# Null key's tables after the first entry's queries, in a decoder's cross-attention on one core

## The chip, the cores and the metric

The kernel runs on one core of a Trainium2 chip. The metric is device microseconds (us) of one launch on that core; lower is better. The engines are named as the profile names them: PE (TensorE, matrix products; PEld is its weight load), DVE (VectorE), ACT (ScalarE), POOL (GpSimd) and SP (SyncE, which here only issues DMAs). Each engine works through its own queue in order and waits at semaphores for the others.

## The reference, cut to what matters

Two decoder layers over 8 entries of 256 tokens with 256 features, float32. The change concerns the cross-attention of layer 1, with 16 heads of 64 and one learned "null" key and value that all heads share:

```python
q = split_heads(layernorm(x) @ Wq)                    # (8, 16, 256, 64)
k, v = split(ctx_2048 @ Wkv)                          # 256 context rows of 512
k = concat(null_kv[0], k); v = concat(null_kv[1], v)  # 257 keys
attn = softmax(q * 64**-0.5 @ k.T)
out = (attn @ v) @ Wout                               # 1024 -> 256
x = x + layernorm(out) * ln_scale + ln_bias
```

Before it stand layer 0 (self-attention with 16 heads of 16, a cross-attention, experts that choose their tokens) and layer 1's causal self-attention; behind it a feed-forward layer with one expert per token and a shared expert.

## The kernel before, in words

Everything is one program on one core. The tokens stay on the chip as `x`, 16 tiles of 128 tokens. A first stage works through 24 attention units (layer 0's self- and cross-attentions, layer 1's self-attentions) in an order written out by hand for all five engines (`order_of_jobs`, opened with `manual_schedule(engines=PINNED)`). Its last lines also make the first entry's keys and values for the heads of 64 (`keys_x`, `vals_x`; tiles kTx and vx), because these need only the context. The stage takes its on-chip memory from two pools (`pads`, `work` there called "aw") and its PSUM banks from three ("amm", "asc", "ao").

Then `order.close()` ends the hand-made order. Where no order is pinned, the framework's scheduler places each instruction on its engine's queue by program order and by when its inputs and its memory are free.

`tables_x` (called at L1085) makes three tables that all entries use, in tiles of a pool that lives to the end:

- `wn`: the query weights times the null key, summed over each head's 64 (DVE: two products `byk`, L829, four reductions, L836), so that the null key's scores are one product with the normalised tokens;
- `nvw`: the null value times the output weights, a row for each head. `nvs` holds for each pair of heads c (8 of them) a 128 x 128 block that is zero but for two columns; 8 products of 128 x 128 by 256 add up in one bank (L854), and DVE copies it out (L855);
- `hot8`: a table of ones for the sums of the weights.

`byk` and `nvs` are scratch tiles, in the slots of the tag "pT" of the pool that `work` names at that point.

After that the first stage's pools are closed (`first.close()`, `banks.close()`), and new ones are opened where those lay: "d2" for the work tiles, "wsum" for sums of weights, and the PSUM pools "xmm" (3 banks), "xsc", "xo".

`null_cross_attention` then makes entry 0's queries and runs over the 8 entries. For entry 0: `layernorm_T` (statistics, the norm `xn` on DVE, four PE transposes into PSUM, ACT's copy to `xnT`), `sums_of_weights` (DVE, L1406, tiles tw and twq: sums of blocks of the key, value and query weights, from which later entries' seven-product scheme takes its operands), `null_key` (two products with `wn`, then the exponential `en` on ACT), and `features` (the queries `qTx`: 16 products of 128 x 128 by 256, each in two halves of 64 columns by `product`, L272, four banks named fm, each copied out by the `copy` that is handed in). Then, for each entry, `weighted` computes scores (`stx`, L1513), exponentials (`pTx`, L1517), sums of weights (`den`, L1528) and weighted values (`ox`, L1553), while the next entry's keys, values and queries are made by `seven` (k7, v7, q7), and `outward` applies `wout_x` and adds `en` times `nvw`. From the second half of entry 0 on PE's order is again pinned.

A float32 product shows as two PE instructions in the trace. In a row such as "128*64 128x256" the first pair is contraction by weight columns, the second the moving operand. `product4` (L278) splits a product into four groups of 32 columns.

Of the kernel before, what the change touches and what calls it, by code (L numbers as in the profile page):

```python
# [43 lines left out]
HP = 32  # L44
CTX = 512
XH, XD = 16, 64
# [111 lines left out]
def plain(  # L158
# [4 lines left out]
    nc = tc.nc  # L163
# [79 lines left out]
    def norm_stats(views, eps, pool, tag):  # L243

        n = len(views)
        st = pool.tile([P, 2, 6], F32, tag=f"{tag}st", name=f"{tag}st")
        mv = pool.tile([P, 2, 2], F32, tag=f"{tag}mv", name=f"{tag}mv")
        for i, v in enumerate(views):
            nc.vector.bn_stats(st[:, i, :], v)
            nc.vector.bn_aggr(mv[:, i, :], st[:, i, :])  # L250
        ve = pool.tile([P, 2], F32, tag=f"{tag}ve", name=f"{tag}ve")
        nc.vector.tensor_scalar(ve[:, :n], mv[:, :n, 1], eps, None, ALU.add)  # L252
        rs = pool.tile([P, 2], F32, tag=f"{tag}rs", name=f"{tag}rs")
        nc.gpsimd.tensor_tensor(rs[:, :n], ve[:, :n], mhalf[:, :n], ALU.pow)  # L254
        return mv, rs

    def normed(dst, src, mv, rs, i, engine=nc.vector):
        return engine.tensor_scalar(dst, src, mv[:, i, 0:1], rs[:, i : i + 1], ALU.subtract, ALU.mult)

    def layernorm_T(b, work, mm, bufs=2):  # L260

        xn = work.tile([P, 2, D], F32, tag="xn", name="xn", bufs=bufs)
        mv, rs = norm_stats([x[:, 2 * b + t, :] for t in range(2)], 1e-5, small, "ln")
        for t in range(2):
            last = normed(xn[:, t, :], x[:, 2 * b + t, :], mv, rs, t)
        return last, transposed(xn, work, mm, "xnT", bufs=bufs)
# [3 lines left out]
    def product(out, lhsT, rhs, start, stop):  # L270
        return [
            nc.tensor.matmul(out[h], lhsT[:, h], rhs, start=start, stop=stop, skip_group_check=True)  # L272
            for h in (slice(0, 64), slice(64, P))
        ]
# [7 lines left out]
    def transposed(rows, work, mm, tag, dst=None, bufs=2):  # L282

        ps = mm.tile([P, 2, 2 * P], F32, tag="mm", name="tr")
        for t in range(2):
            for c in range(2):
                nc.tensor.transpose(ps[:, c, t * P : (t + 1) * P], rows[:, t, c * P : (c + 1) * P], ident)
        if dst is None:
            dst = work.tile([P, 2, 2 * P], F32, tag=tag, name=tag, bufs=bufs)
        nc.scalar.copy(dst, ps)  # L290
        return dst
# [285 lines left out]
    work = first.enter_context(tc.tile_pool(name="aw", bufs=2))  # L577
    banks = ExitStack()
    mm = banks.enter_context(tc.tile_pool(name="amm", bufs=3, space=PSUM))
# [214 lines left out]
    nc8 = XH // 2  # L794
# [24 lines left out]
        nc.sync.dma_start(lnb, a["L1_xattn_ln_bias"].rearrange("(o d) -> o d", o=1).to_broadcast([P, D]))  # L819
        return wd, ctxs, kvs, wproj, wkv_x, wq_x, wout_x, nkrow, nvcol, lns, lnb  # L820

    def tables_x(wd, wq_x, wout_x, nkrow, nvcol):


        wn = wd.tile([P, 2, 2, XD], F32, name="wn")
        nc.gpsimd.memset(wn, 0.0)
        for k in range(2):
            byk = work.tile([P, XH, XD], F32, tag="pT", name="byk", bufs=4)
            nc.vector.tensor_tensor(  # L829
                byk,  # L830
                wq_x[:, k, :].rearrange("p (h d) -> p h d", d=XD),
                nkrow.unsqueeze(1).to_broadcast([P, XH, XD]),
                ALU.mult,
            )
            for i in range(2):
                nc.vector.tensor_reduce(  # L836
                    wn[:, k, :, HP * i : HP * i + nc8 // 2],
                    byk.rearrange("p (c i g) d -> p i g c d", i=2, g=2)[:, i],
                    AX.X,
                    ALU.add,  # L840
                )

        own = wd.tile([P, 2], F32, name="own")
        nc.vector.tensor_reduce(own, ident.rearrange("p (g w) -> p g w", g=2), AX.X, ALU.add)
        nc.vector.tensor_tensor(own, own, nvcol.to_broadcast([P, 2]), ALU.mult)
        nvs = work.tile([P, nc8, P], F32, tag="pT", name="nvs", bufs=4)
        nc.gpsimd.memset(nvs, 0.0)
        for c in range(nc8):
            at = HP * (c % 2) + c // 2
            nc.vector.tensor_copy(nvs[:, c, at : at + XD + 1 : XD], own)  # L850
        nvw = wd.tile([P, D], F32, name="nvw")
        ps = mm.tile([P, 2, S], F32, tag="mm", name="nvw")
        for c in range(nc8):
            nc.tensor.matmul(ps[:, 0, :], nvs[:, c, :], wout_x[:, c, :], start=c == 0, stop=c == nc8 - 1)  # L854
        nc.vector.tensor_copy(nvw, ps[:, 0, :])  # L855

        hot = wd.tile([P, nc8, HP], F32, name="hot8")
        nc.gpsimd.memset(hot, 0.0)
        for i in range(2):
            nc.gpsimd.memset(hot.rearrange("p c w -> p (c w)")[:, HP * i : nc8 * HP : 2 * HP + 1], 1.0)  # L860
        return wn, nvw, hot
# [6 lines left out]
    def key_room():  # L868
        return kvs.tile([P, nc8, S], F32, tag="kT", name="kTx")

    def value_room():
        return kvs.tile([P, 2, XH, XD], F32, tag="vx", name="vx")
# [157 lines left out]
    order = ExitStack()  # L1030
# [19 lines left out]
    for n, u in enumerate(units):  # L1050
# [14 lines left out]
        for k in range(4):  # L1065
# [7 lines left out]
            if (n, k) == (20, 1):  # L1073
                for left in ex:
                    assert next(left, None) is None
                wd, ctxs, kvs, wproj, wkv_x, wq_x, wout_x, nkrow, nvcol, lns, lnb = weights_x()
# [5 lines left out]
    for i in (2, 3):  # L1082
        vals_x(kv0[1], ctxT0, i)
    order.close()
    wn, nvw, hot8 = tables_x(wd, wq_x, wout_x, nkrow, nvcol)  # L1085
    first.close()
    banks.close()
    banks = ExitStack()
    mm = banks.enter_context(tc.tile_pool(name="xmm", bufs=3, space=PSUM))
# [280 lines left out]
    def null_cross_attention(phase):  # L1370
        work = phase.enter_context(tc.tile_pool(name="d2", bufs=2))
# [3 lines left out]
        def features(dst, w, rows, copy):  # L1375
            n = w.shape[1]
            for c2 in range(0, nc8, 2):
                ps = mm.tile([P, 2, S], F32, tag="mm", name="fm")
                for i in range(2):
                    for cc in range(n):  # L1380
                        product(
                            ps[:, i, :], w[:, cc, (c2 + i) * P : (c2 + i + 1) * P], rows[:, cc, :], cc == 0, cc == n - 1
                        )
                copy(dst[:, c2 : c2 + 2, :], ps)

        def query_room():
            return work.tile([P, nc8, S], F32, tag="qT", name="qTx", bufs=1)
# [13 lines left out]
        def sums_of_weights(blocks, which):  # L1401
            ((b11, b12), (b21, b22)), (t1, t2, t3, t4) = blocks
            for dst, p, q in ((t1, b12, b11), (t2, b22, t1), (t4, b21, t2), (t3, b22, b12))[which]:
                for c in range(dst.shape[1]):
                    for m in range(dst.shape[2]):
                        nc.vector.tensor_tensor(dst[:, c, m], p[:, c, m], q[:, c, m], ALU.subtract)  # L1406
# [90 lines left out]
        def null_key(xnT):  # L1497
            nps = mm.tile([P, 2, S], F32, tag="mm", name="nps")
            for k in range(2):
                product(nps[:, 0, :], wn[:, k].rearrange("p g w -> p (g w)"), xnT[:, k, :], k == 0, k == 1)  # L1500
            en = work.tile([P, S], F32, tag="en", name="en")
            nc.scalar.activation(en, nps[:, 0, :], AF.Exp, scale=scale)
            return en
# [134 lines left out]
            return hidden_seven(q, shared["of_w"], sx, mm, pair, spare)  # L1638


        _, xnT = layernorm_T(0, work, mm, 1)
        (kT, v), qT = kv0, query_room()
        sums_of_weights(kv_blocks, slice(0, 3))
        sums_of_weights(q_blocks, slice(0, 3))
        en = null_key(xnT)
        features(qT, wq_x, xnT, nc.vector.tensor_copy)
        for blocks in (kv_blocks, q_blocks):
            sums_of_weights(blocks, slice(3, 4))
        load_router()
        order = ExitStack()  # L1650
        for b in range(B):
# [4 lines left out]
            if more:  # L1656
                _, xnT = layernorm_T(b + 1, work, mm, 1)
# [17 lines left out]
            if more:  # L1675
                of_x = sums_of_rows(xnT, 1, "swq", True)
                kT, v, qT = key_room(), value_room(), query_room()
# [24 lines left out]
            if more:  # L1702
# [4 lines left out]
                en = null_key(xnT)  # L1707
# [15 lines left out]
    with ExitStack() as phase:  # L1723
        null_cross_attention(phase)
# [1217 lines left out]
```

## Time and profile before

| | us |
|---|---|
| median of 3 runs | 1150.59 |
| lowest, highest | 1148.03, 1150.82 |
| the profiled execution | 1146.4 |
| its span, first to last instruction | 1144.7 |
| mean granted PE clock | 0.993 |

| engine | busy us in the span | share |
|---|---|---|
| PE | 1106.4 | 97% |
| DVE | 581.4 | 51% |
| ACT | 444.9 | 39% |
| POOL | 418.8 | 37% |

Times in rows are us from the span's start. A row of a timeline gives start, duration, engine, line, operation, what is written from what is read, shapes and count; in brackets stands the idle time of the engine before it, and what ended that. The chain of waits is the work that ended last, followed back from the last instruction; its rows give start, duration and what. Rows of stretches give for each stretch its length, then busy time (and instructions) of PE, PEld, DVE, ACT and POOL, then the granted PE clock, the DMA engines' busy share and GB/s. The edited part lies between 420 and 450 us.

### The profile page before, as it was taken

The page shows a single profiled execution, that of the slowest core. Times are in us where ns is not written, and L with a number is a line of the kernel's source. Part 1 is how long each engine was busy: PE and PEld are TensorE (multiplying, and loading weights), DVE is VectorE, ACT ScalarE, POOL GpSimd, SP SyncE. Part 2 cuts the span into 40 slices and gives each one's busy share as a digit, 9 for nine tenths or more (in the row PEclk, how much of TensorE's full clock was granted, in tenths as well). Part 3 has the DMA queues.
Part 4 walks back from the last instruction along what each step waited for, and adds up shares of the span by engine and source line. Part 5 has one row for each costly group of instructions (what it writes and reads, how often), then busy time and mean ns, then how long its engine had stood idle before and what let it go on. Part 6 is the DMA issues. An engine that isn't in the chain of part 4 may idle for free.

```text
span 1144.7 us, 33720 instructions
## 1 busy us (share of the span) xinstructions
PE 1106.4 (97%) x14690; PEld 704.9 (62%) x14690; DVE 581.4 (51%) x1577; ACT 444.9 (39%) x699; POOL 418.8 (37%) x480
## 2 busy tenths in 40 slices
PE   6979999999999999999999999999999999999997
PEld 3434455555555445767676767676765667888874
DVE  5557889899878447343433333332324573222213
ACT  4757776656444432232323323232414220222320
POOL 2427366446677422324141414142425223000014
PEclk9989999999999999999999999999999999999999
DMA  8073333231103200101010101010103026799934
GB/s 246 2 240 121 105 107 96 71 112 54 37 11 143 109 3 19 40 19 39 20 40 19 39 20 40 19 39 19 40 20 95 1 94 262 312 415 386 390 107 141
DMA packets 52253, 117.15 MB, mean 102 GB/s; under 512 B 8816, under 2 KB 37216, under 8 KB 47744
## 3 DMA queue, kind: packets, MB, share of 16 engines
q1 hardware_dynamic: 45920, 99.17, 25.4%
q0 software_dynamic: 3456, 12.73, 3.1%
q10 hardware_dynamic: 2720, 3.02, 0.7%
q8 instruction: 117, 1.92, 0.7%
q14 instruction: 40, 0.33, 0.1%
HBM read 104.26 MB, written 27.93 MB: 115 GB/s over the span
## 4 chain that ended last, share of the span: by engine, by line
PE 86%; DVE 6%; ACT 3%; issue 1%; SPq 1%; DMA 1%; POOL 1%; ACTq 0%; DVEq 0%; POOLq 0%
PE h L272 7%; PE st L330 7%; PE k L272 7%; PE v L272 6%; PE wo L272 5%; PE o L367 5%; PE ox L1553 5%; PE stx L1513 5%; PE out L1930 4%; PE out L1747 4%; PE qk L278 3%; PE h L1161 3%; PE q L272 3%; ACT pT L341 2%; PE ao L278 2%; PE v L278 2%
## 5 line engine op out<-in xcount | busy, mean ns | idle before, releaser
L341 ACT ACTIVATE pT<-st 128x1024 f32<-128x1024 f32 (+1 forms) x128 | 110.5, 915 | 74.2 <-PE st L330 70.3
L367 PE MATMUL o<-pT,padv 128*32 128x256 f32 (+1 forms) x1536 | 96.4, 367 | 7.0 <-DVE by_q L383 5.5
L1519 POOL TENSOR_TENSOR both<-pTx 128x512 f32<-128x512 f32 x64 | 81.5, 1298 | 27.1 <-issue 23.8
L272 PE MATMUL h<-xrT,w 128*64 128x128 f32 (+1 forms) x1936 | 87.1, 250 | 0.5 <-issue 0.5
L272 PEld LDWEIGHTS h<-xrT,w 128*64 128x64 f32 x1936 | 84.6, 137 | 3.4 <-issue 1.1
L341 ACT ACTIVATE pT<-st,kbias 128x1024 f32<-128x1024 f32 x64 | 67.9, 1112 | 36.0 <-PE st L330 36.0
L1154 DVE TENSOR_TENSOR midr<-sl,h 128x128 f32<-128x128 f32 x102 | 29.4, 288 | 100.7 <-PE h L272 67.5
L367 PEld LDWEIGHTS o<-pT,padv 128*32 128x32 f32 x1536 | 44.6, 110 | 54.4 <-issue 18.9
L1517 ACT ACTIVATE pTx<-stx 128x1024 f32<-128x1024 f32 x64 | 62.1, 1022 | 40.7 <-PE stx L1513 35.7
L1153 ACT ACTIVATE sl<-h 128x128 f32<-128x128 f32 (+1 forms) x114 | 35.4, 311 | 94.8 <-PE h L272 55.8
L330 PE MATMUL st<-qm,kT 32*128 32x512 f32 (+1 forms) x512 | 67.3, 594 | 3.7 <-DVE seq L513 2.2
L254 POOL TENSOR_TENSOR lnrs<-lnve,mhalf 128x2 f32<-128x2 f32 x48 | 35.8, 749 | 91.8 <-DVE lnve L252 84.9
L278 PE MATMUL qk<-xnT,l_wqkv 128*32 128x256 f32 x1024 | 68.5, 391 | 0.0
L1513 PE MATMUL stx<-qTx,kTx 64*128 64x256 f32 x512 | 64.3, 391 | 2.5 <-ACT pTx L1517 2.5
L1553 PE MATMUL ox<-pTx,vx 128*32 128x256 f32 x1024 | 62.3, 380 | 0.0
L1608 POOL TENSOR_TENSOR oT<-oT,rs 128x512 f32<-128x512 f32 x30 | 37.7, 1287 | 65.7 <-DMA rs<-rd 65.7
L1513 PEld LDWEIGHTS stx<-qTx,kTx 64*128 64x128 f32 x512 | 46.1, 186 | 20.7 <-ACT pTx L1517 7.2
L272 PE MATMUL wo<-wout_x,oT 128*64 128x256 f32 x512 | 58.0, 379 | 0.0
L346 POOL TENSOR_SCALAR_AFFINE_SELECT pT<-pT 128x512 f32<-128x512 f32 x64 | 42.1, 672 | 41.4 <-ACT pT L341 41.1
L254 POOL TENSOR_TENSOR lxrs<-lxve,mhalf 128x2 f32<-128x2 f32 x8 | 5.6, 704 | 133.5 <-DVE sc L1292 103.3
L278 PEld LDWEIGHTS qk<-xnT,l_wqkv 128*32 128x32 f32 x1024 | 32.9, 113 | 26.9 <-issue 8.7
L1930 PE MATMUL out<-w,midr 128*64 128x256 f32 x408 | 47.5, 379 | 0.7 <-issue 0.7
(365 smaller groups left out, 2154.8 us busy)
## 6 DMA issues: line engine op xcount, KB each, us to landing
w<-packs SPq DMA_DIRECT2D x22, 1408.0 KB
w<-packs SPq DMA_DIRECT2D x22, 768.0 KB
rs<-rd SPq DMA_DIRECT2D x16, 512.0 KB
packs<-L_ffn_w_eDF SPq DMA_DIRECT2D x8, 704.0 KB
packs<-L_ffn_w_eDF SPq DMA_DIRECT2D x8, 640.0 KB
packs<-L_ffn_w_eFD SPq DMA_DIRECT2D x8, 640.0 KB
wkv_x<-L_xattn_Wkv POOLq DMA_DIRECT2D x1, 4096.0 KB, 16.9
ctxT<-ctx_T SPq DMA_DIRECT2D x8, 512.0 KB
```

The lines of the kernel that those rows point to most:

```text
L272: nc.tensor.matmul(out[h], lhsT[:, h], rhs, start=start, stop=stop, skip_group_check=True)
L278: nc.tensor.matmul(out[h : h + HP], lhsT[:, h : h + HP], rhs, start=start, stop=stop, skip_group_check=True)
L330: nc.tensor.matmul(st[:, r, :, :n], self.kT[rows, c, bass.ts(kt, P)], self.qm[rows, :, c, q0:], start=True, stop=True,)
L341: nc.scalar.activation(pT[:, :, :, :n], st[:, 2 * k : 2 * k + 2, :, :n], AF.Exp, scale=self.scale, **kb)
L346: nc.gpsimd.affine_select(out=pT[:, :, :, :P], in_=pT[:, :, :, :P], compare_op=ALU.is_ge, fill=0.0, base=0, pattern=[[0, 2], [0, 2], [1, P ...
L367: nc.tensor.matmul(o[HP * j : HP * j + HP, m, q0:], self.v_pad[:, kt, 8 * c + 2 * j + m, :], pTs[j // 2][:, j % 2, m, : S - q0], start=kt ...
L1513: nc.tensor.matmul(st[:, g, kt, :], kT[rows, c, bass.ts(kt, P)], qT[rows, c, :], start=True, stop=True)
L1517: nc.scalar.activation(pT, st, AF.Exp, scale=scale)
L1519: nc.gpsimd.tensor_tensor(both, pT[:, :, 0, :], pT[:, :, 1, :], ALU.add)
L1553: nc.tensor.matmul(o[at : at + HP, i, :], v[:, kt, 2 * (c2 + i) + g, lo : lo + HP], pT[:, g, kt, :], start=kt == 0, stop=kt == 1, skip_gro ...
L1747: nc.tensor.matmul(ps, mid[:, i, lo : lo + P], w2[:, i, :], start=i == 0, stop=i == NFC - 1)
L1930: nc.tensor.matmul(ps[h], mid[:, i, h], sets[k % len(sets)][1][:, i, :], start=i == 0, stop=i == NFC - 1, skip_group_check=True,)
```

## The change

- `tables_x` is called inside `null_cross_attention`, after entry 0's norm and queries, and takes that stage's `work` and `mm`; so `byk` and `nvs` are tiles of "d2" and nvw's bank is one of "xmm".
- The products for `nvw` write only the 32 rows in which a pair's block is not zero: for each c two products of 128 x 32 by 256, for g = 0 and 1, at rows 64 g + 32 (c mod 2). Sixteen products of 32 columns take the place of eight of 128.
- Entry 0's queries are copied out of PSUM by ACT, not by DVE.
- In program order it is now: norm, queries, tables, null key, and then the sums of weights, which stood ahead of the null key and the queries. PE's order is pinned over norm, queries, tables and null key.

```diff
-    def tables_x(wd, wq_x, wout_x, nkrow, nvcol):
+    def tables_x(wd, wq_x, wout_x, nkrow, nvcol, work, mm):
...
         ps = mm.tile([P, 2, S], F32, tag="mm", name="nvw")
         for c in range(nc8):
-            nc.tensor.matmul(ps[:, 0, :], nvs[:, c, :], wout_x[:, c, :], start=c == 0, stop=c == nc8 - 1)
+            for g in range(2):
+                at = XD * g + HP * (c % 2)
+                nc.tensor.matmul(
+                    ps[at : at + HP, 0, :],
+                    nvs[:, c, at : at + HP],
+                    wout_x[:, c, :],
+                    start=c < 2,
+                    stop=c >= nc8 - 2,
+                    skip_group_check=True,
+                )
         nc.vector.tensor_copy(nvw, ps[:, 0, :])
...
     order.close()
-    wn, nvw, hot8 = tables_x(wd, wq_x, wout_x, nkrow, nvcol)
     first.close()
...
+        order = ExitStack()
+        order.enter_context(tc.manual_schedule(engines={mybir.EngineType.PE}))
         _, xnT = layernorm_T(0, work, mm, 1)
         (kT, v), qT = kv0, query_room()
+        features(qT, wq_x, xnT, nc.scalar.copy)
+        wn, nvw, hot8 = tables_x(wd, wq_x, wout_x, nkrow, nvcol, work, mm)
+        en = null_key(xnT)
+        order.close()
         sums_of_weights(kv_blocks, slice(0, 3))
         sums_of_weights(q_blocks, slice(0, 3))
-        en = null_key(xnT)
-        features(qT, wq_x, xnT, nc.vector.tensor_copy)
         for blocks in (kv_blocks, q_blocks):
             sums_of_weights(blocks, slice(3, 4))
```

## The prediction

> **What bounds the kernel now.** I read the page first: TensorE (PE) is busy 97% of the span, and the chain that ended last is 86% PE.
>
> ```profile
> PE 1106.4 (97%) x14690; PEld 704.9 (62%) x14690; DVE 581.4 (51%) x1577; ACT 444.9 (39%) x699; POOL 418.8 (37%) x480
> ```
>
> So an edit is worth what it takes off PE's row of work or out of a gap in it, and I looked for the place in the chain in order of time. The edited stretch runs from the last product of the first stage's values (vps, end 432.95) to the first score (stx):
>
> ```profile
> 425.01 1.07 PE ao L278 x16
> 426.09 6.87 PE vps L278 x64
> 432.95 3.67 PE nvw L854 x16
> ...
> 437.64 0.64 PE tr L287 x4
> ...
> 438.43 0.59 ACT xnT L290
> ...
> 439.07 1.09 PE nps L272 x8
> 440.16 8.59 PE fm L272 x64
> 448.75 1.09 PE stx L1513 x8
> ```
>
> It is 448.75 - 432.95 = 15.80 us long, and all of it is on the path: nvw 3.67, a gap of 1.04 (VectorE (DVE) copies nvw, then norms), transposes 0.64, a gap of 0.79 (ScalarE (ACT) copies xnT), null key 1.09, queries 8.59.
>
> The queries look too long: elsewhere 72 instructions of the same form (wo, 64 columns by 256) take 7.79 us in the chain, 108 ns each; here 64 take 8.59, 134 each. The busy time by stretches, with the granted clock in the column after POOL, says why:
>
> ```profile
> 286.42:289.83 3.41, 1.94 (x46) 1.19 (x42) 2.38 (x8) 0.30 (x1) 2.27 (x3) 1.00 0.71 251
> 368.34:371.75 3.41, 2.04 (x32) 0.73 (x24) 2.91 (x7) 1.61 (x4) 3.40 (x4) 1.00 1.02 428
> 433.20:436.61 3.41, 3.40 (x16) 2.66 (x14) 0.00 (x0) 0.41 (x1) 0.00 (x0) 1.00 0.45 154
> 436.61:440.02 3.41, 1.58 (x14) 1.08 (x16) 3.38 (x7) 0.59 (x1) 0.00 (x0) 1.00 0.01 2
> 440.02:443.43 3.41, 3.41 (x20) 1.95 (x18) 3.41 (x7) 0.38 (x1) 0.00 (x0) 0.50 0.00 0
> 443.43:446.84 3.41, 3.41 (x34) 2.26 (x32) 3.41 (x7) 0.00 (x0) 0.00 (x0) 1.00 0.02 5
> ```
>
> After a stretch with PE busy 1.58 of 3.41 us, the clock is 0.50 for 3.41 us. (The trace's other halvings under load begin at 20.18 and 78.21, and both lie a whole number of 3.413 us before 440.02, so I read the trace in such frames.) That costs 3.41/2 = 1.7 us of the queries; 64 at 108 ns would be 6.9. Stretches of the same length with one gap of about 1.5 us (busy 1.94 and 2.04) were not followed by it.
>
> Last, who stands in whose way (the timelines of PE, DVE, ACT and GpSimd (POOL)):
>
> ```profile
> 415.40 3.66 PE L278 MATMUL fm<-ctxT,wkv_x 128*32 128x256 f32 x64
> ...
> 425.01 1.07 PE L278 MATMUL ao<-l_wo,attT 128*32 128x256 f32 x16 [0.35 <-DVE attT L393]
> ...
> 420.02 1.23 DVE L829 TENSOR_TENSOR byk<-wq_x,nkrow 128x1024 f32<-128x1024 f32 x1 [4.30 <-PE o L367]
> ...
> 436.64 0.42 DVE L855 COPY nvw<-nvw 128x256 f32<-128x256 f32 x1 [9.36 <-PE nvw L854]
> ...
> 433.02 0.59 ACT L893 COPY vx<-vps 128x512 f32<-128x512 f32 x1 [2.85 <-PE vps L278]
> ...
> 426.41 0.81 POOL L1133 DMA_DIRECT2D router<-L_ffn_router_DE  x1 [4.98 <-PE ao L278]
> ```
>
> DVE idles 9.36 us before the nvw copy although the weight sums (tw, L1406) need only weights that have long been loaded: tw and xn lie where the first stage's pools were, and the last reader of those is the nvw product itself (nvs is a tile of the old pool). The router's tile, of a pool opened in the same way, was released by the last ao at 426.1. So without nvs in the old pool, I take 426.1 as the time from which tiles of the new pools can be written.
>
> **The change part by part.**
>
> *Norm, transposes and queries first.* The norm (0.73 for both halves, statistics long there) runs at about 427 instead of 436.98: the 1.04 gap before the transposes is gone. What is late next is the PSUM bank: the transposes' pool opens when the old one closes, and its last user is ACT's copy of vps, 433.02 + 0.59 = 433.61. I take 433.67 as their start, 0.72 after vps; if a bank that came free earlier suffices, 0. Then as before: 0.64 and the gap of 0.79 for the xnT copy. Queries: 64 x 108 ns = 6.9 at full clock, 8.6 if it is halved again. Idle in the new stretch is 0.72 + 0.79 = 1.5 of any 3.41 us, busy 1.9, which is the size of the two stretches without a halving (1.94, 2.04) and not of the one with it (1.58); I take full clock.
>
> [...]
>
> *nvw as products of 32 columns.* 16 instructions of 128 columns (3.67) become 32 of 32 columns, in four column groups side by side. The row with that form, fm at L278, has 64 in 3.5 to 3.66 us, 55 ns each: 32 x 55 = 1.8. The row den (8 in 0.57 between scores of another form, 71 ns each) gives 2.3. It is one run of 32, nearer to fm, so 1.9 with something for the change of form at both ends.
> [...]
>
> *Null key after nvw.* 8 instructions, 0.86 to 1.09 in the chain; in the later entries, with PE running on, 0.86. I take 0.95. It needs wn, nvw's product needs nvs: both come from DVE's tables, moved out of the old pool. There they were interleaved with the last attention unit (420.02 to 427.3); now they cannot start before 426.1. Two byk at 1.22, four reductions at 0.64, eight copies in 0.73 are 5.7 us; with the x addition (0.68) and the norm (0.73) ahead of them they end at 426.3 + 7.1 = 433.4. POOL's memset of nvs (0.95) goes beside. Needed is nvs at about 441.6: cover of 8 us. If that cover is gone, PE waits (rival 2).
>
> *The tables leave the last unit's DVE chain.* byk at 420.02 held by_q back, and attT came late for ao: 0.35 us of PE idle. Without it, -0.35 (bound: 0 if something else fills DVE).
>
> *ACT copies the queries.* Four copies of 0.59 (the vx row) where DVE had four of 0.69. ACT idles 9.27 us there; three lie beside the next products, the last beside nvw. Nothing on the path: 0. Behind them in ACT's queue stand only en and the first exponentials, which come later in any case. DVE loses 2.8 us of work. Its weight sums (12 x 0.62, 3 x 0.6, 3.6, 1.8 = 14.6) start at about 433.5 instead of 437.6, so what the next entry needs comes earlier than before; it was not late before (first k products at 466.04 without a wait).
>
> No DMA is added or moved: the router load and the next context (issued when vps ends, 433.4) stay where they are. On SP's queue nothing is passed.
>
> *Sum, on the profiled execution.* From vps's end: 0.72 + 0.64 + 0.79 + 6.9 + 1.9 + 0.95 = 11.9 against 15.80, which is -3.9; with the 0.35, **-4.2 us**. Of that 1.7 is the clock, 1.8 nvw, the rest gaps. After stx PE is the path to the end (in the chain from 973 to 1138 there are two gaps, 0.70 and 0.54), so the shift should reach the end. The profiled execution took 1146.4 (span 1144.7 and 1.7 around it): 1142.2. The runs' median of 1150.59 lies 4.2 above it; the same saving on it gives **1146.4**, -0.37%.
>
> **The rivals.**
> 1. *The clock is halved again.* For: busy 1.9 of 3.41 counts the transposes' 0.64; were they not counted, it is 1.26, and before 0.95, so the limit could lie between 1.26 and 1.9. Against: the low stretch must fall whole into one of the 3.41 us frames; in this trace's frames (433.20 to 436.61) only part of it would. Price 1.7: 1148.1. Chance 0.13.
> [...]
> 2. *PE waits for the tables* (slower). If DVE, once the old pool is free, runs the weight sums ahead of the tables, nvs is ready at 427.7 + 12.8 + 5.7 = 446.2 instead of 433.4; PE, through at 441.6, idles 4.6 us and the clock halves over nvw and null key (+1.4 to 1.7): stx at 446.2 + 1.9 + 0.95 + 1.6 = 450.7, 1.9 later than before: 1152.5. With the sums on wq_x or the next norm ahead too it is over 1154. It decides from nvs later than about 445. Against: the tables stand ahead of the sums in the program. Chance 0.08.
> 3. *The gain is swallowed later.* The DMA queues are full from 1000 to 1050 (share 1.00), and DVE's and POOL's order in the later entries may come out otherwise. Against: the expert loads are released by PE's own progress, and PE hardly waits. 1150. Chance 0.10.
> 4. *The transposes need not wait* for ACT's copy: -4.9, 1145.7. Chance 0.12.
>
> **How the numbers follow.** The forecast has 0.57, rivals as above. About 0.3% (3.4 us) is what a measurement of this kernel can tell from no change. The forecast lies 0.8 us beyond that, and single runs differ by 2.8, so of forecast and rival 4 (0.69) I count 0.57 as faster and 0.12 as same; rival 1 gives 0.03 faster and 0.10 same, rival 3 0.02, 0.06 and 0.02, rival 2 0.02 same and 0.06 slower. Together: faster 0.62, same 0.30, slower 0.08. The forecast's own range is 1145 to 1148 (bounds: bank, den's rate, 0.35); with the runs' scatter downward and rivals 1 and 3 upward, 1143.6 to 1150.6.
>
> **What would show it.** In the changed profile: the transposes about 0.7 us after vps's end; queries 64 in about 6.9 at clock 1.00; no PE wait before nvw's 32 instructions, about 1.9; stx about 4.2 earlier than 448.75; DVE's tables at 427 to 434 and its idle time before the nvw copy gone or filled with tw; ao without its 0.35. Wrong would be a clock of 0.50 in 437 to 445, PE waiting for DVE before nvw, or later entries longer than the 58.6 us that they take from one null key to the next (505.72 to 564.28 in the chain).

## The result and the profile after

The changed kernel took 1146.46 us (median of 6 runs, 1145.15 to 1147.57) beside 1151.13 for the kernel before (6 runs, 1148.03 to 1154.73): on record as a ratio of 0.9964, 95% interval 0.9946 to 0.9982, or 4.1 us less, give or take 2 (the two medians as they stand lie 4.7 apart). The prediction was 1146.4.

The profiled execution of the changed kernel has a span of 1143.9 us, only 0.8 less than before's 1144.7, so the two profiles have to be compared by parts. The page's first part:

```profile
PE 1100.9 (96%) x14706; PEld 702.4 (61%) x14706; DVE 575.6 (50%) x1573; ACT 447.2 (39%) x703; POOL 419.3 (37%) x480
```

PE is busy 5.5 us less, with 16 instructions more. That is more than the edited stretch gained, because time at half clock shows as busy too (3.41 of 3.41 us at a clock of 0.50 from 440.02 on in before's profile), and a halving near 20 us is in before's profile alone. The edited stretch in PE's timeline, first before:

```profile
425.90 7.05 PE L278 MATMUL vps<-wkv_x,ctxT 128*32 128x512 f32 x64
...
448.68 2.00 PE L1513 MATMUL stx<-qTx,kTx 64*128 64x256 f32 x16
```

and after:

```profile
423.50 7.05 PE L278 MATMUL vps<-wkv_x,ctxT 128*32 128x512 f32 x64
431.25 0.66 PE L287 MATMUL tr<-ident,xn 128*128 128x128 f32 x4 [0.71 <-ACT vx L902]
432.70 7.13 PE L272 MATMUL fm<-xnT,wq_x 128*64 128x256 f32 x64 [0.80 <-ACT xnT L290]
439.76 1.93 PE L856 MATMUL nvw<-wout_x,nvs 128*32 128x256 f32 x32
441.63 1.08 PE L272 MATMUL nps<-xnT,wn 128*64 128x256 f32 x8
442.64 1.57 PE L1521 MATMUL stx<-qTx,kTx 64*128 64x256 f32 x12
```

The transposes wait for ACT's copy of vx, as foreseen; between queries, nvw and null key PE does not wait. From the end of vps (423.50 + 7.05 = 430.55) to the first stx it is 12.09 us; by the same rows before's was 448.68 - (425.90 + 7.05) = 15.73. DVE's timeline shows the tables after the norm and the weight sums in the time that was idle:

```profile
424.35 1.91 DVE L258 TENSOR_SCALAR xn<-x,lnmv,lnrs 128x256 f32<-128x256 f32 x2
426.18 2.35 DVE L829 TENSOR_TENSOR byk<-wq_x,nkrow 128x1024 f32<-128x1024 f32 x2
428.46 2.45 DVE L836 TENSOR_REDUCE wn<-byk 128x8 f32<-128x512 f32 x4
430.83 0.64 DVE L850 COPY nvs<-own 128x2 f32<-128x2 f32 x8
431.39 2.48 DVE L1414 TENSOR_TENSOR tw<-wkv_x 128x512 f32<-128x512 f32 x4
```

The clock by stretches of 3.41 us stays at 1.00:

```profile
428.13:431.54 3.41, 2.70 (x27) 0.81 (x20) 3.41 (x14) 0.59 (x1) 0.00 (x0) 1.00 0.01 2
431.54:434.95 3.41, 2.62 (x26) 1.65 (x26) 3.41 (x6) 0.84 (x2) 0.00 (x0) 1.00 0.48 154
434.95:438.36 3.41, 3.41 (x34) 2.25 (x32) 3.41 (x7) 1.13 (x3) 0.00 (x0) 1.00 0.00 0
```

Where the rest of the span went, from marks in PE's rows, named after the tiles that they write (the o products at 81 and 79 us that wait for by_q, vps's end, the first stx, the counts of the routing, the experts' first xrp, the last shared h, PE's end):

| part | before | after | difference |
|---|---|---|---|
| start to o | 81.12 | 78.97 | -2.15 |
| o to vps's end | 351.83 | 351.58 | -0.25 |
| vps's end to first stx | 15.73 | 12.09 | -3.64 |
| stx to counts | 473.20 | 473.19 | -0.01 |
| counts to first xrp | 48.59 | 48.59 | 0.00 |
| routed experts | 138.22 | 141.00 | +2.78 |
| last quarter | 29.51 | 29.50 | -0.01 |
| after PE's end | 6.50 | 8.98 | +2.48 |

The change shows in the second and third lines. The others vary between executions of any kernel here: over 13 profiles (this one, before's, and eleven of the experiments), "start to o" is 79.0 to 79.3 or 80.6 to 81.7, "routed experts" 137.4 to 142.8 and "after PE's end" 6.2 to 9.4, while "stx to counts" is 473.15 to 473.21 in all. The first of these goes with the clock: the seven profiles with a halving near 20 us have 80.6 to 81.7, the six without one 79.0 to 79.3.

### The profile page after: what moved, and what is told of

Same layout as the page of the kernel before. It is cut to its first block, busy times and chain, and to the rows that moved or that the text cites. A ratio compares the mean times of both kernels' runs of the same rounds, so it can differ in the third digit from the quotient of the medians.

```text
span 1143.9 us, 33749 instructions
## 1 busy us (share of the span) xinstructions
PE 1100.9 (96%) x14706; PEld 702.4 (61%) x14706; DVE 575.6 (50%) x1573; ACT 447.2 (39%) x703; POOL 419.3 (37%) x480
## 5 line engine op out<-in xcount | busy, mean ns | idle before, releaser
L1569 DVE COPY oT<-ox 128x512 f32<-128x512 f32 x16 | 11.1, 691 | 78.9 <-PE ox L1561 78.9
L383 DVE STREAM_TRANSPOSE by_q<-o 128x512 f32<-128x512 f32 x48 | 34.0, 708 | 33.0 <-PE o L367 33.0
```

## The experiments

Ratios are to the kernel before, run beside on the same chip. The stretch from vps's end to the first stx is read from one profile each.

| kernel | stretch, us | ratio (95% interval) |
|---|---|---|
| before, first profile (clock halved in it) | 15.73 | |
| before, second profile | 15.12 | |
| before + filler products | 15.12 | 0.9999 (0.9987 to 1.0011) |
| before + ACT copies | 14.04 | 0.9989 (0.9978 to 1.0000) |
| before + 32 columns | 13.22 | 0.9985 (0.9968 to 1.0002) |
| before + both | 12.14 | 0.9982 (0.9961 to 1.0002) |
| change, nvw of 128 columns | 13.88 | 0.9977 (0.9962 to 0.9992) |
| change, DVE copies | 12.09 | 0.9987 (0.9973 to 1.0001) |
| change, sums ahead of tables | 12.16 | 0.9975 (0.9961 to 0.9988) |
| change, second profile | 12.10 | 0.9970 (0.9956 to 0.9984) |
| change, nvw ahead of queries | 11.08 | 0.9958 (0.9944 to 0.9973) |

The intervals are 2.5 to 4.7 us wide; most steps between neighbours are smaller, so it is the stretch that tells the parts apart, and the ratios only show that no part does great harm elsewhere.

**The change once more.** No edit.

> The changed kernel once more, to see what repeats. Theory A (the gain sits in the edited stretch): from the end of the last vps to the first stx it takes 12.1 us again (before: 15.8 in the one profile, 14.1 if the clock is not halved there), the transposes 0.7 after vps, queries 7.0 at clock 1.00, and the median is 4 to 5 us below the kernel before. PE's waits put down to 'issue' in the expert stage (3.9 us in the first profile, 1.2 before) differ from run to run. Theory B (the edited stretch gains 3.7 but the expert stage always gives back 2.5 of it): those waits come to 3.5 to 4 again and the median is 1 to 2 us below before.

The stretch came out at 12.10, as theory A had it, and the ratio at 0.9970, 3.4 us, which is less than theory A's 4 to 5 and more than theory B's 1 to 2 (the interval reaches from 1.8 to 5.1). The waits for "issue" in the expert stage were 4.2 us here, as theory B wanted; in the other kernels with the new order they are 1.0 to 4.0, with the old one 0.3 to 2.3. "Routed experts" takes 139.7 on a mean of the seven profiles of the new order (137.8 to 142.8) and 138.2 of the six of the old (137.4 to 139.3). After PE's end it is 8.6 beside 7.6. Whether these 1.5 and 1.0 us are chance is not settled by so few. The totals speak against a lasting loss: stretch and ao save 3.3 to 4.0, a ratio of 0.9971 to 0.9965, and measured were 0.9964 and 0.9970; with 1.5 us given back it would be 0.998. The six ratios of kernels in the new order come to 3.2 us of saving on a mean, and their stretches, with 0.3 for ao, to 3.2 as well. One of these waits shows what it may cost further:

```profile
1014.48 4.47 PE L1942 MATMUL out<-w,midr 128*64 128x256 f32 x24 [2.17 <-issue]
```

```profile
1011.06:1014.47 3.41, 1.25 (x44) 1.16 (x40) 0.83 (x3) 0.55 (x2) 0.00 (x0) 1.00 1.04 392
1014.47:1017.88 3.41, 3.40 (x17) 2.65 (x18) 0.00 (x0) 0.00 (x0) 0.00 (x0) 0.50 0.98 408
```

PE was busy 1.25 us of a frame, and the next ran at half the clock. That execution's span is 1148.5.

**One part alone: 32 columns.**

```diff
-            nc.tensor.matmul(ps[:, 0, :], nvs[:, c, :], wout_x[:, c, :], ...)
+            for g in range(2): ...   # the change's products, rest as before
```

> The kernel before with one part of the change alone: nvw as products of 32 columns, all else in the old order. Theory A: nvw 3.7 becomes 1.9, the gaps of 1.04 and 0.79 stay; from vps to stx 14.0 if the clock is halved over the queries, 12.3 if not; the median 1.8 us below before. Rival: the nvw product was covered (something else sets when the transposes start), then the stretch stays at 15.8 (or 14.1) and the median does not move.

```profile
432.55 1.91 PE L856 MATMUL nvw<-wout_x,nvs 128*32 128x256 f32 x32
...
437.86 5.35 PE L272 MATMUL fm<-xnT,wq_x 128*64 128x256 f32 x48
444.07 1.95 PE L272 MATMUL fm<-xnT,wq_x 128*64 128x256 f32 x16 [0.86 <-DVE qTx L1393]
445.95 2.00 PE L1522 MATMUL stx<-qTx,kTx 64*128 64x256 f32 x16
```

nvw is on the path and takes 1.9. But at full clock the stretch was 13.22, not 12.3: the last 16 instructions of the queries waited 0.86 for a bank that DVE had to copy out, and DVE was in its weight sums: thirteen of them (twelve tw, one twq) stand ahead of the first copy in its queue, as DVE's rows of the filler run show below. The halved clock in before's first profile had hidden that wait. This is the point that the prediction did not have.

**The order without the 32 columns.** The changed kernel with the old line for nvw.

> The change without its new form of nvw: eight products of 128 columns, in the new order and with ACT's copies. Theory A: nvw 3.7, the rest as in the changed kernel: 13.9 from vps to stx, clock 1.00, median 1.8 above the changed kernel, some 2.5 below before. Rival (the order gains nothing but the clock, and that by chance): 13.9 as well, but before's stretch shows 14.1 in other runs, and the median equals before within 0.15%.

```profile
439.68 3.72 PE L854 MATMUL nvw<-wout_x,nvs 128*128 128x256 f32 x16
```

13.88, as expected. To the changed kernel it is 1.79 more, the price of the old form. The medians differ by 1.1, less than they scatter.

**The new order with DVE's copies.**

```diff
-        features(qT, wq_x, xnT, nc.scalar.copy)
+        features(qT, wq_x, xnT, nc.vector.tensor_copy)
```

> The change with the queries copied by DVE as before, in the new order. Theory A: the copies are covered on either engine: 12.1 to 12.4 from vps to stx, median within 1 us of the changed kernel; DVE's sums end 2.8 later, without anyone waiting. Rival: DVE, with tables and weight sums in its queue, gives the banks back late: PE waits for qTx between the queries or ahead of nvw, 1 us or more, and the stretch is 13 or more.

```profile
431.32 2.48 DVE L1414 TENSOR_TENSOR tw<-wkv_x 128x512 f32<-128x512 f32 x4
433.73 2.48 DVE L1414 TENSOR_TENSOR tw<-wkv_x,tw 128x512 f32<-128x512 f32 x4
436.14 0.68 DVE L1392 COPY qTx<-fm 128x512 f32<-128x512 f32 x1
```

12.09: in the new order the engine that copies does not matter to the path. Now that the weight sums stand behind the queries in the program, only eight of them lie ahead of the first copy in DVE's queue. That copy ends at 436.82, some 1.2 us before the last group of the queries can start (about 438.0: the queries begin at 432.64 in this profile, and their first 48 instructions take 5.35 in the rows of the 32-column run above). The median was 1.1 us above the second run of the change; the intervals overlap.

**A filler in the gap of before.**

```diff
         nc.vector.tensor_copy(nvw, ps[:, 0, :])
+        fill = op.tile([P, 2, S], F32, tag="o", name="fill")
+        for _ in range(2):
+            nc.tensor.matmul(fill[:, 0, :], ident, wout_x[:, 0, :], start=True, stop=True)
```

> The kernel before with two products of 128 columns whose result nobody reads, put behind nvw so that PE is busy 0.9 us of the 1.04 us gap; the clock cannot fall there. Theory A (as predicted, the halving costs 1.7): 15.8 - 1.7 = 14.1 us from the end of vps to the first stx, median 1.7 below before in those runs where before is halved. Theory C (from the run with nvw of 32 columns in the old order, where the last queries waited 0.86 us for DVE's copy): at full clock the queries run into DVE's queue, the last group starts when DVE has made the first copy, some 9.5 us after nvw, and the stretch is 15.0; so the halving costs only 0.8.

```profile
435.02 1.03 PE L859 MATMUL fill<-wout_x,ident 128*128 128x256 f32 x4
436.22 0.63 PE L287 MATMUL tr<-ident,xn 128*128 128x128 f32 x4 [0.18 <-issue]
...
444.77 1.95 PE L272 MATMUL fm<-xnT,wq_x 128*64 128x256 f32 x16 [0.86 <-DVE qTx L1388]
```

```profile
436.21 2.49 DVE L1410 TENSOR_TENSOR tw<-wkv_x 128x512 f32<-128x512 f32 x4
438.62 4.90 DVE L1410 TENSOR_TENSOR tw<-wkv_x,tw 128x512 f32<-128x512 f32 x8
443.43 0.68 DVE L1410 TENSOR_TENSOR twq<-wq_x 128x512 f32<-128x512 f32 x1
444.04 0.68 DVE L1388 COPY qTx<-fm 128x512 f32<-128x512 f32 x1
```

Theory C: 15.12 at full clock, with the same wait of 0.86, and no gain over before (ratio 0.9999). So the halving, when it happens, costs the stretch 15.73 - 15.12 = 0.6, not 1.7.

**Before with ACT's copies.** `features(qT, wq_x, xnT, nc.scalar.copy)` in the old place.

> The kernel before with one part of the change alone: entry 0's queries copied by ACT, old order, nvw of 128 columns. Theory C: no wait for qTx; 14.2 from vps to stx at full clock, 15.8 if the clock is halved over the queries, median 0.8 or less below before. Theory A (ACT's copies are worth nothing by themselves, the halving is all): the same stretch as the run with the filler.

```profile
440.53 7.08 PE L272 MATMUL fm<-xnT,wq_x 128*64 128x256 f32 x64
447.54 2.00 PE L1513 MATMUL stx<-qTx,kTx 64*128 64x256 f32 x16
```

The queries run through in 7.0 and the stretch is 14.04: ACT's copies take 1.08 off the old order.

**Before again.** No edit.

> The kernel before once more, one look. Theory C (the halving is a matter of where the 3.41 us frames fall, and without it DVE's copies hold the queries): with frames that do not hold both gaps, clock 1.00 over the queries, a wait of 0.86 for qTx ahead of the last queries, 15.0 us from vps to the first stx; if both gaps fall into one frame, 15.7 again. Theory A (always halved): 15.7 whatever the frames are.

```profile
435.04:438.45 3.41, 1.87 (x16) 1.30 (x18) 3.41 (x8) 0.70 (x2) 0.00 (x0) 1.00 0.01 2
438.45:441.86 3.41, 3.41 (x36) 2.25 (x34) 3.41 (x7) 0.27 (x1) 0.00 (x0) 1.00 0.02 5
```

```profile
444.33 1.95 PE L272 MATMUL fm<-xnT,wq_x 128*64 128x256 f32 x16 [0.86 <-DVE qTx L1384]
446.21 2.00 PE L1513 MATMUL stx<-qTx,kTx 64*128 64x256 f32 x16
```

Theory C again: no halving, the wait for DVE in its place, 15.12. The frames lie only a little otherwise. By the halving near 78, one begins 3.95 us after vps's end here, and 3.66 after it in the first profile. The first gap begins 3.65 after vps's end in both, so a shift of 0.3 put 0.3 us of it into the frame before, and PE was busy 1.87 instead of 1.58. This profile is the fairer "before".

**Both small parts without the order.** The kernel before with the 32 columns and ACT's copies.

> The kernel before with two parts of the change, 32 columns and ACT's copies, but in the old order. Theory C: 15.0 - 1.75 - 0.9 = 12.3 to 12.4 from vps to stx at full clock, 14.0 if halved; with the 0.35 of the last ao that stays, the median 0.6 above the changed kernel when not halved, and on a mean over frames about 1. Theory A (the order is worth 2 us by itself): 14 in any case.

```profile
436.95 7.08 PE L272 MATMUL fm<-xnT,wq_x 128*64 128x256 f32 x64
443.95 2.00 PE L1522 MATMUL stx<-qTx,kTx 64*128 64x256 f32 x16
```

12.14 from vps to stx. At full clock the new order itself is worth 0.05 in this stretch, and the 0.35 at the last ao, which is still there in this kernel. The time, 1144.18 against 1147.23 on that chip, does not separate it from the change.

**The weight sums ahead of the tables.** In the program the weight sums stand ahead of the tables:

```diff
         features(qT, wq_x, xnT, nc.scalar.copy)
+        sums_of_weights(kv_blocks, slice(0, 3))
+        sums_of_weights(q_blocks, slice(0, 3))
         wn, nvw, hot8 = tables_x(wd, wq_x, wout_x, nkrow, nvcol, work, mm)
...
         order.close()
-        sums_of_weights(kv_blocks, slice(0, 3))
-        sums_of_weights(q_blocks, slice(0, 3))
```

> The changed kernel with the sums of weights ahead of the tables in the program (DVE's order turned round, nothing else): the rival of the prediction in which PE waits for the tables. Worked out from the changed profile: xn ends 4.3 us before vps does, then sums 8.1 and tables with two sums between 6.9, so nvs is ready some 10.7 after vps's end, 1.4 later than PE wants it: 13.5 from vps to stx, median 1.4 above the changed kernel, no halving. The prediction's figure for that case was 4.6 of waiting. Rival: no wait, because the tables' own work is short: 12.1.

```profile
440.72 0.22 DVE L850 COPY nvs<-own 128x2 f32<-128x2 f32 x2
442.05 0.50 DVE L850 COPY nvs<-own 128x2 f32<-128x2 f32 x6
```

```profile
441.81 2.00 PE L856 MATMUL nvw<-wout_x,nvs 128*32 128x256 f32 x32
```

The expectation of 13.5 was wrong. The tables did come late, but the first two blocks of nvs were ready at 440.9 and the others by 442.55, while PE worked on the first: the products need nvs block by block, and took 2.00 in place of 1.93. Cover of 8 us was used up for 0.07 us.

**A longer gap.** ACT copies xnT of entry 0 three times.

```diff
+        for _ in range(spare):      # 2 for entry 0
+            nc.scalar.copy(dst, ps)
         nc.scalar.copy(dst, ps)
```

> The changed kernel with xnT of entry 0 copied three times by ACT (the first two are overwritten), which makes the gap ahead of the queries 1.2 us longer. Theory (clock goes down for the next frame when PE is busy less than about half of a frame of 3.41 us): 13.3 from vps to stx if the gaps lie in two frames, 15.0 with clock 0.50 if about 1.75 us of idle time fall into one frame, which is so for three positions of the frames in four; the frames can be read from the halving near 78. [...]

```profile
436.58 7.13 PE L272 MATMUL fm<-xnT,wq_x 128*64 128x256 f32 x64 [2.03 <-ACT xnT L292]
```

```profile
18.28:21.69 3.41, 1.54 (x16) 0.54 (x18) 3.24 (x12) 2.35 (x5) 0.89 (x2) 1.00 1.09 361
21.69:25.10 3.41, 3.41 (x32) 1.35 (x30) 1.09 (x5) 1.94 (x2) 0.70 (x1) 0.50 1.07 371
...
434.70:438.11 3.41, 1.53 (x14) 1.06 (x16) 3.41 (x7) 1.76 (x3) 0.00 (x0) 1.00 0.40 141
438.11:441.52 3.41, 3.41 (x34) 2.30 (x32) 3.41 (x7) 1.17 (x2) 0.00 (x0) 1.00 0.00 0
```

13.32, and no halving, although 1.88 us of idle time fell into one frame. In the same execution the frame at 18.28, busy 1.54, was followed by one. So my limit was drawn too high, and it is not sharp in PE's busy time. Nor does the length of a single gap sort them: the longest here was 2.03 and none followed, while before was halved after gaps of 1.04 and 0.79, and the second run of the change behind a wait of 2.17.

**A further version: nvw ahead of the queries.** The changed kernel with the tables' line ahead of the queries, so that nvw's products fill the gap in which ACT copies xnT.

> The changed kernel with the tables (nvw's products) ahead of the queries on PE, so that they lie in the gap in which ACT copies xnT. Theory A: 0.8 less: 11.3 from vps to stx, PE without a wait between transposes and queries, since nvs is ready (431.5 in the first profile) before the transposes end (431.9); median 0.8 below the changed kernel. Rival: the products wait for nvs or for nvw's bank, the queries start later than before: 12 or more.

```profile
431.10 0.66 PE L287 MATMUL tr<-ident,xn 128*128 128x128 f32 x4 [0.71 <-ACT vx L902]
431.68 1.93 PE L856 MATMUL nvw<-wout_x,nvs 128*32 128x256 f32 x32
433.55 7.13 PE L272 MATMUL fm<-xnT,wq_x 128*64 128x256 f32 x64
440.51 1.03 PE L272 MATMUL nps<-xnT,wn 128*64 128x256 f32 x8
441.47 2.00 PE L1521 MATMUL stx<-qTx,kTx 64*128 64x256 f32 x16
```

No wait between transposes and queries, 11.08 us, 1.0 below the change, and the lowest ratio of all, 0.9958 (1144.93, of five runs, against 1149.81). Its interval overlaps the change's; the gain over it is shown by the rows, not by the times.

## Why the prediction was right, point by point

**The stretch.** Forecast 11.9, measured 12.09: the bank's wait 0.72 foreseen, 0.71; the copy's gap 0.79, 0.80; queries 6.9, 7.06 to the next instruction; nvw 1.9, 1.87; null key 0.95, 1.01. With the change of form at both ends, nvw's 32 came to 1.87 where 32 x 55 ns is 1.76, so the change of form has room for about 0.1 us in these rows.

**The 0.35 of ao.** It went, since nothing but the attention unit stood in DVE's queue; from o to vps's end 0.25 was saved in the pair of profiles.

```profile
421.77 1.91 PE L278 MATMUL ao<-l_wo,attT 128*32 128x256 f32 x32
```

**The release of memory.** The reading that the new pools are free from the last ao on was right: xn began when the x addition had ended, and the tables ended at 431.5, 0.9 after vps; the prediction's figures gave 433.4 with vps at 432.6, 0.8 after it. (The norm took 1.91, not 0.73; POOL's memset of nvs, 0.98 from 424.82 on, fell into that time, but no row shows whether it was the cause. The rest took a little less.)

**The term that was mis-sized: the clock.** The sum took 1.7 us for it. Two things were wrong in that step. First, whether before is halved there went with where the frames fell: it was in one profile of two (PE busy 1.58 of the frame with the gaps, against 1.87 in the other), and in none of three other kernels in the old order with the same gaps (1.93 to 2.03). From the start of the first gap to the end of the second it is 2.47 us, so a frame of 3.41 would hold both in (3.41 - 2.47)/3.41 = 28% of positions, were all as likely. They are not: a frame begins 0.2 to 0.7 us after vps's end in the six profiles of the old order, and 1.0 to 1.5 after it in the seven of the new one. So how often before is halved stays open. Second, at full clock before waits 0.86 for DVE's copy, so the halving costs 0.6 and not 1.7. The change's gain in the stretch is thus 3.0 where before is not halved and 3.6 where it is, with 0.25 to 0.35 ahead of it.

**The term that was taken as nothing: who copies the queries.** The prediction put it at 0, since the first profile shows no wait for DVE's copies; but that was at half clock. At full clock they cost 1.08 in the old order. The new order and ACT's copies each remove that wait (12.09 with either engine in the new order, 12.14 with ACT in the old); the change does both. Its gain at full clock is thus 1.8 for nvw's form, 1.1 for the wait, and 0.1 of gaps. The forecast had 1.8 for nvw, 1.7 for a clock and 0.3 to 0.4 of gaps: nearly the same sum for a partly wrong reason, and in that part luck. The median agreed to 0.1 us, which is luck too: stretch and ao say 3.3 to 4.0, and the two measurements 4.1 and 3.4, each give or take 1.6 to 2.

**The rivals.** The clock was not halved again in any of the five profiles with the change's own gaps. But in none of them did both gaps fall into one frame, as the prediction had counted (busy 1.9): they fell into two, busy 2.7 and 2.6 us, so these profiles do not test that case. Frames busy 1.64 to 2.0 elsewhere were never followed by a halving. PE did not wait for the tables even when these were made late. The gain reached the counts of the routing whole: stx to counts is the same to 0.06 us in all kernels. Behind them the profiles scatter too much to tell, and the ratios show no loss. The transposes did wait for ACT's copy.

## What to carry to other kernels

A chain taken from one execution with a halved clock hides the wait that comes next (here 0.86 us for qTx): before the clock is counted as a gain, look at which buffer the slow stretch was waiting for anyway. Where several small parts remove the same wait, price them by adding each alone and leaving each out; here the order and the copies were worth 1.1 us once, not twice. And where total times scatter by 4 us, fixed marks in the critical engine's rows can separate 0.1 us: the stretch came out at 12.09 and 12.10, and at 15.12 twice.

## What the runs showed of the hardware

Between 10 and 1100 us the halved clock (0.50) lasts 3.41 us or twice that (6.83 near 78 us). Where a profile has several halvings, they begin on a raster of 3.41 us: 20.18, 78.21 and 440.02 in before's first profile lie 17 and 106 times 3.413 us apart, 79.22 and 1014.47 in the second run of the change 274 times. The place of the raster changes with the execution (0.55 to 3.11 us into it, counted from the span's start). Before's halving came after gaps of 1.04 and 0.79 us. Over 13 profiles, taken frame by frame by that raster between 10 and 1100 us, all 33 frames with PE busy under 1.5 us (44%) were followed by a halved one, none with 1.6 or more was, and between 1.53 and 1.58 it went both ways. What decides in that band is open; leaving out the transposes does not sort the frames, since 1.25 without any was halved (second run of the change, 1011.06) and 1.87 with 0.66 of them was not (the changed kernel's first profile, 15.11).

A halving at 20 us, in the kernel's start, comes in some executions and not in others in the same way (PE busy 1.26 to 1.54 in the frame ahead in the seven with it, 1.57 to 1.99 in the six without), which is where 2 us between the two first profiles came from. Waits of 0.2 to 2.2 us for "issue" in the expert stage, at a DMA share of about 1.0 (1.04 in the frame above), make up the 2.8 in "routed experts": 1.2 us before, 4.0 after. What PE waits for there, and what the 2.5 us after PE's end are, no row here shows.
